# Reordering the first sample's loads, first norm and weight folds in a fused graph-network kernel

## The chip, the cores and the metric

The kernel runs on one core of a Trainium2 chip. The metric is the device time of one execution in microseconds (us), as the median of several runs: 2542.31 us before the change (three runs, 2541.89 to 2542.35). The profile is that of one such execution (2541.99 us, span in the trace 2540.2 us).

A core has five engines that run side by side: TensorE (matrix products; PE in the profile, PEld for its weight loads), VectorE (DVE), ScalarE (ACT), GpSimd (POOL) and SyncE (SP, which here only issues transfers). Transfers between the memory of the chip and the core's own buffers are done by 16 DMA engines; SP, ACT and POOL can each issue them on a queue of their own. Each engine works through its instructions in the order in which the program gives them, and waits where an operand or a buffer is not ready.

## The reference, cut to what matters

There are 16 samples, each with 1024 nodes of 128 features (`x`) and a dense adjacency matrix of 1024 x 1024 (`adj`), all in fp32. Two parts follow one another, each with a residual and a layer norm:

```python
def first(x, adj, W, b):                      # "first GNN"
    degree = adj.sum(-1)[:, :, None]
    nb = einsum('bid,bij->bjd', x, adj) / degree
    return relu(concat([x, nb], -1) @ W.T + b)

def layer(nodes, adj, ws, bs, wd, bd, wn, bn, wu, bu):
    src = einsum('bjv,bij->biv', nodes @ ws + bs, l2norm(adj, 2))   # rows scaled
    dst = einsum('bjv,bji->biv', nodes @ wd + bd, l2norm(adj, 1))   # columns scaled
    return tanh(concat([src, nodes @ wn + bn, dst], 2) @ wu + bu)

x = layernorm(x + first(x, adj, W, b))
y = x; # four such layers follow; the third and fourth also read earlier layers' inputs
x = layernorm(x + four_layers(y, adj, ...))
```

`l2norm(adj, 2)` divides each row by the root of its sum of squares, `l2norm(adj, 1)` each column. The layers' weights `ws`, `wd`, `wn` are multiplied with the parts of `wu` once ("folded"), so that messages come out of one product per layer.

## The kernel before

Samples are worked off one after another. While TensorE is in the layers of one sample, the next sample's adjacency is loaded, its sums of squares and degrees are taken, its columns and rows scaled and its first GNN and norm done. Sample 0 has nobody to hide behind: its loads, sums, first GNN and first norm stand at the start of the program, and the folding of the weights lies in its first layer. The last sample's final norm stands at the end. The change concerns these two ends and sample 0's first two layers.

The start: loads, then sums and gathers by pairs of row blocks (each pair is 1 MB, each of its four transfers 256 KB).

```python
load_pair(nc.scalar, PAIRS[0], range(G))
load_nodes(1)                                  # SP's queue
load_pair(nc.scalar, PAIRS[1], range(2))
load_pair(nc.sync, PAIRS[1], range(2, G))
load_nodes(0)
load_pair(nc.sync, PAIRS[2], range(G))
nc.sync.dma_start(w0n, w0)
nc.sync.dma_start(b0c, ...)
load_pair(nc.sync, PAIRS[3], range(G))
fetched = [fetch_weights(raw, 0, nc.sync, wm)]
rows = {...}                                   # rows 2, 3 of the adjacency once more, in another layout
fetched += [fetch_weights(raw, l, nc.sync) for l in range(1, NL)]
rows[0] = load_rows(0, 0, ...); rows[1] = load_rows(0, 1, ...)
make_identity(nc, ident)
# ...
for h in (1, 0):                               # transposes of x: both halves ahead of the gathers
    ...
for h, k in PAIRS[:-1]:
    for i in range(h * BPH + k, h * BPH + k + 2):
        square(i)                              # ScalarE, with the row's sum of squares
        degree(i)                              # VectorE, row sum
        if i != BPH:
            add_square(i)                      # GpSimd, adds squares for the column sums
        for h2 in (1, 0):
            gather(h2, i)                      # TensorE: matmul(pa[h2], xn[:, i], a[:, i, half(h2)])
```

The end of the first GNN and the first norm:

```python
def first_weights(b, h, xT, agT, yT, order=..., back=...):
    pw = product(f"pw0_{b}_{h}")
    by_halves(pw, w0T[:, 0], xT[:, s], True, False)
    by_halves(pw, w0T[:, 1], agT[:, s], False, True)
    nc.scalar.activation(order(yT[:, s]), back(pw), AF.Relu, bias=b0c)

degree_row(1)
with_x(1); with_x(0)                           # x into the norm's banks, by an identity product
square(first); square(second)                  # the last two row blocks, 2 and 3
for h in (1, 0):
    gather(h, first); gather(h, second)
degree(first); scaled(1); degree(second); degree_inverses(0)
add_square(first)
# power of the rows' sums of squares, on GpSimd
first_weights(0, 1, ...)
degree_row(0); scaled(0)
with_y(1)                                      # four small products add relu's result
first_weights(0, 0, ...)
stats = {1: norm_stats(pn[1], range(BPH), "0_0_1")}
fold_begin(0, fetched[0], nc.vector.tensor_copy)
with_y(0)
fold_end(0, fetched[0])
rinv = row_inverses(0, inv)
shift = norm_shift(stats[1], BPH, "0_0_1")
for q in range(BPH):
    norm_write_act(x1n[:, BPH + q], pn[1][:, q], stats[1], shift, q)
stats[0] = norm_stats(pn[0], range(BPH), "0_0_0")
add_square(second)
to_x1(1)                                       # transposes and a copy
for q in range(BPH):
    norm_write(x1n[:, q], pn[0][:, q], stats[0], q)
to_x1(0)

def norm_stats(pn, blks, name):
    for q in range(n):
        nc.vector.bn_stats(...); nc.vector.bn_aggr(...)
    nc.vector.tensor_scalar_add(ve, variance, LN_EPS)
    nc.gpsimd.tensor_tensor(rstd, ve, mhalf, ALU.pow)      # to the power -1/2
    return mv, rstd
```

Layer 1 of sample 0 runs on unscaled data and has hooks ahead of numbered steps. Steps 0 and 1 are own products, 2 to 17 the products with the columns, 18 to 33 those with the rows (`at`, which VectorE transposes from `rows`). Layer 2 has hooks too:

```python
hooks = {1: lambda *_: inverses(0, st0, NB), 3: rows0, 5: folded(1, fold_begin), 7: cinv0,
         9: folded(1, fold_end), 10: second0, 18: first0, 19: folded(2, fold_begin),
         22: folded(2, fold_end), 24: folded(3, fold_begin), 26: sums0, 29: folded(3, fold_end)}
# inverses: column sums from the parts, then their power on GpSimd; cinv0: that inverse as a row, by TensorE
# second0 ends, and first0 begins, with rows 0 and 1: scale_rows on ScalarE, transpose_rows on VectorE
# sums0: combine_1(y), finish(1), combine(2, y, T), combine_1(yt)

plain_layer(b, 0, ...)
wm = message_weights(b, 1)
a2 = load(n)             # the next sample's adjacency, into the buffer that the raw weights leave

# layer 2
def quarters2(b=b):
    if b == 0:
        combine(3, y, T); combine(2, yt, Q)
    for i in (3, 4):
        combine(i, yt, Q)
hooks = {0: quarters2}   # and sums(n, a2, st, (i,)) of the next sample at eight steps
if b == 0:
    hooks[20] = lambda: combine(4, y, T)
```

`fold_end(l)` ends with a transfer that saves the folded weights; `load(n)` waits until the last save has read the buffer. In `sums`, ScalarE squares a row block into one of two buffers and GpSimd adds it up.

The end of the program, the last sample's norm, first half in two pieces:

```python
shift = norm_shift(stats[1], BPH, ...)
for q in range(BPH):
    norm_write_act(o[:, BPH + q], pn["last"][:, q], stats[1], shift, q)
nc.sync.dma_start(ov[:, BPH:], o[:, BPH:])
for i in pieces:
    for q in range(2):
        nc.tensor.matmul(pn[i][:, q], f4[...], ident, start=False, stop=q == 1)
    stats[0] = norm_stats(pn[i], range(2), ...)
    for q in range(2):
        norm_write(o[:, i + q], pn[i][:, q], stats[0], q)
    nc.sync.dma_start(ov[:, i:i + 2], o[:, i:i + 2])
```

Of the kernel before, what the change touches and what calls it, by code (L numbers as in the profile page):

```python
# [23 lines left out]
def adj_resnorm_kernel(ctx: ExitStack, tc: tile.TileContext, x, adj, w0, b0, layers, out):  # L24
# [230 lines left out]
    def column_sums(b, state):  # L255

        tr = two.tile([P, N], F32, tag="sq", name=f"acct{b}")
        nc.vector.transpose(tr, state["acc"])  # L258
        part = two.tile([P, K], F32, tag="part", name=f"part{b}")
        nc.vector.reduce_sum(part, tr.rearrange("p (k r) -> p k r", r=C), axis=AX.X)  # L260
        state["part"] = part
# [114 lines left out]
    def norm_stats(pn, blks, name):  # L376
# [9 lines left out]
        rstd = two.tile([P, BPH], F32, tag="rst", name=f"rs{name}")  # L386
        nc.gpsimd.tensor_tensor(rstd[:, :n], ve[:, :n], mhalf[:, :n], ALU.pow)
        return mv, rstd

    def norm_write(dst, pn, stats, q):  # L390
        mv, rstd = stats
        nc.vector.tensor_scalar(dst, pn, mv[:, q, 0:1], rstd[:, q:q + 1], op0=ALU.subtract, op1=ALU.mult)

    def norm_shift(stats, n, name):
        mv, rstd = stats
        shift = two.tile([P, BPH], F32, tag="shift", name=f"sh{name}")
        nc.vector.scalar_tensor_tensor(shift[:, :n], mv[:, :n, 0], -1.0, rstd[:, :n], op0=ALU.mult, op1=ALU.mult)
        return shift

    def norm_write_act(dst, pn, stats, shift, q):  # L400
        nc.scalar.activation(dst, pn, AF.Identity, bias=shift[:, q:q + 1], scale=stats[1][:, q:q + 1])
# [23 lines left out]
    def first_weights(b, h, xT, agT, yT, order=lambda v: v, back=lambda v: v):  # L425
# [4 lines left out]
        nc.scalar.activation(order(yT[:, s]), back(pw), AF.Relu, bias=b0c)  # L430
# [4 lines left out]
    def load_rows(b, q, st):  # L435
# [3 lines left out]
        for g in range(G):  # L439
            for h in range(NH):  # L440
                nc.sync.dma_start(st[g * C:(g + 1) * C, :, h * P:(h + 1) * P], v[h, g])
# [266 lines left out]
    def load_nodes(h):  # L708
        for g in range(G):
            nc.sync.dma_start(xn[g * C:(g + 1) * C, h * BPH:(h + 1) * BPH], xv[h][g])  # L710

    load_pair(nc.scalar, PAIRS[0], range(G))
    load_nodes(1)
    load_pair(nc.scalar, PAIRS[1], range(2))
    load_pair(nc.sync, PAIRS[1], range(2, G))
    load_nodes(0)
    load_pair(nc.sync, PAIRS[2], range(G))
    nc.sync.dma_start(w0n, w0)
    nc.sync.dma_start(b0c, b0.rearrange("(p o) -> p o", o=1))
    load_pair(nc.sync, PAIRS[3], range(G))  # L720
    raw = Raw()
    wm = message_tile("wm1_0")
    fetched = [fetch_weights(raw, 0, nc.sync, wm)]
    Q = combined(0, "Q")
    rows = {q: load_rows(0, q, Q[i].rearrange("p k (u c) -> p (k u) c", u=2)) for i, q in ((2, 2), (3, 3))}
    fetched += [fetch_weights(raw, l, nc.sync) for l in range(1, NL)]
    rows[0] = load_rows(0, 0, Q[4].rearrange("p k (u c) -> p (k u) c", u=2))
    rows[1] = load_rows(0, 1, one.tile([P, 2 * NJ, HW // 2], F32, tag="T2", name="rows1_0"))

    make_identity(nc, ident)  # L730
# [9 lines left out]
    for h in (1, 0):  # L740
        pt = product(f"xtr0_{h}")
        for q in range(BPH):
            nc.tensor.transpose(pt[:, q * P:(q + 1) * P], xn[:, h * BPH + q], ident)
        nc.scalar.copy(nodes(xT[:, half(h)]), blocks(pt))

# [27 lines left out]
    for h, k in PAIRS[:-1]:  # L773
        for i in range(h * BPH + k, h * BPH + k + 2):
            square(i)
            degree(i)
            if i != BPH:
                add_square(i)
            for h2 in (1, 0):
                gather(h2, i)  # L780
    pt = product("w0tr")
    for k in range(2):
        nc.tensor.transpose(pt[:, k * P:(k + 1) * P], w0n[:, k * P:(k + 1) * P], ident)
    nc.scalar.copy(w0T.rearrange("p k v -> p (k v)"), pt[:, :2 * P])
    degree_inverses(1)
# [5 lines left out]
    pn = {}  # L791
# [4 lines left out]
    def scaled(h):  # L796
        nc.vector.tensor_mul(agT[:, half(h)], pa[h], dinv[:, half(h)])

# [16 lines left out]

    degree_row(1)
    with_x(1)
    with_x(0)
# [3 lines left out]
    for h in (1, 0):  # L822
        gather(h, first)
        gather(h, second)
    degree(first)
    scaled(1)
    degree(second)
    degree_inverses(0)
    add_square(first)
    nc.vector.tensor_scalar_max(cols[:, :NB], cols[:, :NB], NORM_EPS * NORM_EPS)  # L830
    nc.gpsimd.tensor_tensor(inv[:, :NB], cols[:, :NB], mhalf[:, :NB], ALU.pow)
    first_weights(0, 1, xT, agT, yT, blocks, nodes)
    degree_row(0)
    scaled(0)
    with_y(1)
    first_weights(0, 0, xT, agT, yT, blocks, nodes)
    stats = {1: norm_stats(pn[1], range(BPH), "0_0_1")}
    fold_begin(0, fetched[0], nc.vector.tensor_copy)
    with_y(0)
    fold_end(0, fetched[0])  # L840
    rinv = row_inverses(0, inv)
    shift = norm_shift(stats[1], BPH, "0_0_1")
    for q in range(BPH):
        norm_write_act(x1n[:, BPH + q], pn[1][:, q], stats[1], shift, q)
    stats[0] = norm_stats(pn[0], range(BPH), "0_0_0")
    add_square(second)
# [3 lines left out]
    to_x1(0)  # L850
# [12 lines left out]
    for b in range(B):  # L863
# [9 lines left out]
        if b == 0:  # L873
            for q in (2, 3):
                scale_rows(rows[q], q, rinv)
            t = messages(b, 0, feats, wm, {0: lambda: column_sums(0, st0)}, with_sums=False)
# [12 lines left out]
            def second0(destination, finish):  # L889
# [3 lines left out]
                for q in (0, 1):  # L893
                    scale_rows(rows[q], q, rinv)
# [9 lines left out]
            def sums0(destination, finish):  # L904
# [3 lines left out]
                combine_1(yt)  # L908

# [3 lines left out]
            hooks = {1: lambda *_: inverses(0, st0, NB), 3: rows0, 5: folded(1, fold_begin), 7: cinv0,  # L913
# [246 lines left out]
```

## Time and profile before

| what | value |
|---|---|
| median of three runs | 2542.31 us |
| span in the trace | 2540.2 us |
| TensorE busy | 2500.9 us, 98% |
| VectorE, ScalarE, GpSimd busy | 1646.4, 836.2, 506.2 us |
| moved by the DMA engines | 219.63 MB, mean 86 GB/s |
| SP's queue, ACT's queue | 361696 and 480 packets |
| one row of a 128 x 512 product in a full run of them (gather) | 0.43 us; each fp32 product has two such rows |
| addition of 128 x 1024 on GpSimd | 2.35 us |
| squares of 128 x 1024 on ScalarE, with their sum | 1.05 + 0.19 us |
| row sum of 128 x 1024 on VectorE | 1.22 us |
| power of 128 x 4 and 128 x 8 on GpSimd | 1.01 and 1.65 us |

How to read what follows: in the profile's lines "L771" is a line of the kernel. L771 is the gather, L179 `by_halves`, L490 the messages, L542 the products of layer 1, L669 those of the other layers, L813 the transposes of `to_x1`, L743 the transposes of `x`, L577 a copy of a finished bank on ScalarE, L478 `combine(4, ...)`. "out<-in" are the names of the program's tiles, "x24" is the number of rows merged into the line, and what stands in brackets is the idle time of the engine just before and what ended it. Times are from the start of the span.

### The profile page before, as it was taken

The numbers are of one execution on the slowest core, as the hardware profiler recorded it, in microseconds if no ns is written. First come the engines' busy times: TensorE is split into PE (matmuls) and PEld (weight loads), VectorE is DVE, ScalarE is ACT, GpSimd is POOL, SyncE is SP. The second block draws the span as 40 slices with busy tenths as digits, with TensorE's granted clock in tenths as the row PEclk, the third lists the DMA queues.
The fourth block names the chain that finished last, engine by engine and source line by source line (L and its number), as shares of the span: only waits on it lengthen the run. The fifth ranks groups of instructions, "written<-read, shape, count | busy, mean of one in ns | idle before, by whom it ended". The sixth has DMA issues, their size and how long they took to land.

```text
span 2540.2 us, 30180 instructions
## 1 busy us (share of the span) xinstructions
PE 2500.9 (98%) x11701; PEld 1155.8 (45%) x11701; DVE 1646.4 (65%) x1982; ACT 836.2 (33%) x1552; POOL 506.2 (20%) x192
## 2 busy tenths in 40 slices
PE   7999999999999999999999999999999999999998
PEld 4443545434454444544445444344544445444453
DVE  4657667576675856657576575766758567585643
ACT  4414324143331423315133241433414333142311
POOL 3311303013031120401213021130301203112000
PEclk9999999999999999999999999999999999999999
DMA  9416345172451715436154361634517245271410
GB/s 189 105 38 128 74 91 98 46 141 57 96 106 47 144 41 100 100 69 127 34 108 98 72 117 42 126 72 95 98 43 146 55 96 104 49 143 40 92 23 9
DMA packets 362319, 219.63 MB, mean 86 GB/s; under 512 B 148928, under 2 KB 333504, under 8 KB 362176
## 3 DMA queue, kind: packets, MB, share of 16 engines
q1 hardware_dynamic: 361696, 216.14, 42.0%
q10 hardware_dynamic: 480, 1.57, 0.3%
q8 instruction: 92, 1.51, 0.3%
q14 instruction: 51, 0.42, 0.1%
HBM read 199.17 MB, written 18.46 MB: 86 GB/s over the span
## 4 chain that ended last, share of the span: by engine, by line
PE 64%; DVE 9%; SPq 7%; DMA 7%; POOL 5%; ACT 4%; issue 3%; ACTq 0%; POOLq 0%; DVEq 0%
PE m L669 25%; PE z L669 17%; PE pt L490 9%; PE pa L179 8%; SPq L231 7%; DMA a<-in_adj_dram 4%; POOL acc L252 3%; PE pw L179 2%; POOL inv L292 2%; ACT sq L248 2%; DMA out_dram<-y 2%; DVE e L593 1%; ACT sq L245 1%; DVE acct L258 1%; DVE part L260 1%
## 5 line engine op out<-in xcount | busy, mean ns | idle before, releaser
L369 POOL TENSOR_TENSOR rs<-ve,mhalf 128x32 f32<-128x32 f32 x30 | 162.8, 5428 | 1388.4 <-DVE ve L367 1388.4
L669 PE MATMUL z<-at,t 128*64 128x512 f32 x1224 | 383.7, 592 | 0.0
L669 PE MATMUL m<-Q,S 128*64 128x512 f32 x768 | 339.3, 595 | 2.6 <-ACT e L577 2.6
L669 PE MATMUL m<-T,S 128*64 128x512 f32 x1008 | 290.9, 593 | 0.0
L493 DVE TENSOR_TENSOR t<-pt,wm 128x512 f32<-128x512 f32 x256 | 175.3, 690 | 174.1 <-PE pt L490 174.0
L669 PE MATMUL m<-a,t 128*64 128x512 f32 x1008 | 266.8, 594 | 0.0
L252 POOL TENSOR_TENSOR acc<-acc,sq 128x1024 f32<-128x1024 f32 x90 | 220.4, 2449 | 136.0 <-ACT sq L248 132.5
L669 PE MATMUL z<-a,S 128*64 128x512 f32 x504 | 230.1, 597 | 0.0
L669 PE MATMUL z<-T,t 128*64 128x512 f32 x504 | 226.8, 592 | 2.2 <-DVE T L478 2.2
L669 PE MATMUL z<-a,t 128*64 128x512 f32 x504 | 226.8, 592 | 0.0
L446 ACT ACTIVATE a<-a,rinv 128x256 f32<-128x256 f32 x480 | 198.2, 495 | 57.0 <-DMA a<-in_adj_dram 49.4
L669 PE MATMUL m<-at,t 128*64 128x512 f32 x828 | 214.6, 593 | 0.0
L327 DVE TENSOR_TENSOR a<-a,cinv 128x512 f32<-128x512 f32 x250 | 156.6, 698 | 88.1 <-DMA cinv<-dr 86.2
L490 PE MATMUL pt<-wm,f1T 128*128 128x256 f32 x768 | 213.4, 383 | 0.0
L179 PE MATMUL pa<-a,xn 128*64 128x512 f32 x960 | 208.6, 592 | 0.2 <-DVE e L592 0.2
L669 PE MATMUL z<-at,S 128*64 128x512 f32 x444 | 200.8, 592 | 0.0
L576 ACT COPY e<-m 64x512 f32<-64x512 f32 x63 | 36.7, 582 | 470.4 <-PE m L669 470.1
L669 PEld LDWEIGHTS m<-Q,S 128*64 128x64 f32 x768 | 105.5, 137 | 169.5 <-issue 149.2
L669 PEld LDWEIGHTS z<-at,t 128*64 128x64 f32 x1224 | 120.8, 137 | 130.4 <-issue 111.6
L669 PE MATMUL z<-Q,t 128*64 128x512 f32 x384 | 172.6, 592 | 0.0
L669 PEld LDWEIGHTS m<-T,S 128*64 128x64 f32 x1008 | 102.4, 137 | 144.4 <-issue 124.2
L490 PEld LDWEIGHTS pt<-wm,f1T 128*128 128x128 f32 x768 | 143.3, 190 | 44.0 <-issue 18.3
(189 smaller groups left out, 3675.7 us busy)
## 6 DMA issues: line engine op xcount, KB each, us to landing
a<-in_adj_dram SPq DMA_DIRECT2D x120, 512.0 KB, 12.9
a<-in_adj_dram SPq DMA_DIRECT2D x480, 128.0 KB, 4.2
xn<-in_x_dram SPq DMA_DIRECT2D x128, 64.0 KB, 2.1
wm<-wsave SPq DMA_DIRECT2D x16, 512.0 KB, 3.9
wm<-wsave SPq DMA_DIRECT2D x31, 256.0 KB, 3.1
xs<-in_x_dram SPq DMA_DIRECT2D x60, 128.0 KB, 3.5
cinv<-dr SPq DMA_DIRECT2D x30, 256.0 KB, 5.3
dinv<-dr SPq DMA_DIRECT2D x30, 256.0 KB, 5.2
```

Of the source, the lines that this page charges most:

```text
L179: nc.tensor.matmul(out[s], x[:, s], y, start=start, stop=stop)
L231: nc.sync.dma_start(ov[g, :, ks], ys[g * C:(g + 1) * C, ks])
L248: nc.scalar.activation(sq, a[:, i, :], AF.Square, accum_out=cols[:, i:i + 1])
L252: nc.gpsimd.tensor_add(acc, acc, sq)
L292: nc.gpsimd.tensor_tensor(inv[:, s], cols[:, s], mhalf[:, s], ALU.pow)
L327: engine.tensor_mul(a[:, i, s], a[:, i, s], cinv[:, s])
L369: nc.gpsimd.tensor_tensor(rstd, ve, mhalf[:, :n], ALU.pow)
L446: nc.scalar.activation(st[:, k], st[:, k], AF.Copy, scale=rinv[:, q * QB + k:q * QB + k + 1])
L490: nc.tensor.matmul(pt[:, q], f[:, i * P:(i + 1) * P], wm[:, 1 + c], start=(k == 0), stop=(k == nch - 1))
L493: nc.vector.tensor_add(t[j][:, o:o + 2].rearrange("p k a v c -> p k (a v c)"), pt, wm[:, 0][:, None, :].to_broadcast([P, 2, 2 * P]))
L576: nc.scalar.copy(e0[high], A[high])
L669: nc.tensor.matmul(o, x, y, start=start, stop=stop)
```

## The change

The loads of the first adjacency are halved between SP's queue and GpSimd's queue, all four pairs ahead of everything but the first weights and the nodes; the identity matrix, which GpSimd makes, comes after its eight transfers. Rows 2 and 3 follow with the weights, rows 0 and 1 are issued by GpSimd after the first norm's powers. On TensorE, the products that need only `x` stand ahead of the row blocks, undivided rather than by halves of the output. Folding of layers 2 to 4's weights begins earlier in layer 1, between the scalings of rows 0 and 1 on ScalarE. `combine(3, y, T)` moves from layer 2 into layer 1, and `combine(4, y, T)` from step 20 to step 12 of layer 2. The shift of the norm's writes on ScalarE is computed as minus the mean (VectorE) times the power's result (both on GpSimd). At the end, both pieces' statistics come ahead of their writes. It is meant to let TensorE start earlier, wait less in the first norm and in layer 2, and to shorten the tail. The diff, cut to its core:

```diff
-    load_pair(nc.scalar, PAIRS[0], range(G))
-    load_nodes(1)
     ...
+    nc.sync.dma_start(w0n, w0)
+    for p, pair in enumerate(PAIRS):
+        if p % 2 == 0:
+            load_nodes(1 - p // 2)
+        load_pair(nc.sync, pair, range(G // 2))
+        load_pair(nc.gpsimd, pair, range(G // 2, G))
+    make_identity(nc, ident)
     ...
+    for l, q in enumerate((2, 3, None, None)):
+        fetched.append(fetch_weights(raw, l, nc.sync, None if l else wm))
+        if q is not None:
+            rows[q] = load_rows(0, q, places[q])
     ...
+    to_xT(1)
+    with_x(1)
+    weights_of_x(1)                 # one 128x128 product, w0T[:, 0] with xT
+    for pair in PAIRS[:2]:
+        squares_of(*pair)
+        gathers_of(*pair)
+    nc.vector.tensor_add(sq[6], sq[6], sq[7])
+    add_square(5)
+    add_square(6)
+    to_xT(0)
+    with_x(0)
+    weights_of_x(0)
+    degree_inverses(1)
+    degree_row(1)
+    squares_of(*PAIRS[2])
+    gathers_of(*PAIRS[2])
+    add_square(0)
+    add_square(1)
     square(first)
     square(second)
-    for h in (1, 0):
-        gather(h, first)
-        gather(h, second)
+    gather(1, first)
+    gather(1, second)
     degree(first)
-    scaled(1)
     degree(second)
     degree_inverses(0)
+    degree_row(0)
+    gather(0, first)
+    gather(0, second)
+    scaled(1)
     add_square(first)
     ...
+    add_square(second)
+    weights_of_agT(1)               # w0T[:, 1] with agT, then relu
     scaled(0)
+    weights_of_agT(0)
     with_y(1)
     with_y(0)
+    stats = {1: norm_stats(pn[1], range(BPH), "0_0_1", True)}
+    fold_begin(0, fetched[0])
     fold_end(0, fetched[0])
+    stats[0] = norm_stats(pn[0], range(BPH), "0_0_0")
     for q in range(BPH):
+        norm_write_act(x1n[:, BPH + q], pn[1][:, q], stats[1], q)
+    for q in (0, 1):
+        rows[q] = load_rows(0, q, places[q], nc.gpsimd)
+    acct = column_transpose(0, st0)
     to_x1(1)
     ...                             # to_x1(0), row_inverses, column sums, scaling of rows 2, 3: after the first messages
-            hooks = {1: inverses, 3: rows0, 5: folded(1, fold_begin), 7: cinv0,
-                     9: folded(1, fold_end), 10: second0, 18: first0, 19: folded(2, fold_begin),
-                     22: folded(2, fold_end), 24: folded(3, fold_begin), 26: sums0, 29: folded(3, fold_end)}
+            hooks = {1: inverses, 3: rows0, 4: folded(1, fold_begin), 6: folded(1, fold_end),
+                     7: cinv0, 9: fold_and_scale(2, 0), 11: second0, 12: folded(2, fold_end),
+                     14: fold_and_scale(3, 1), 18: first0, 20: folded(3, fold_end), 26: sums0}
+            # sums0 ends with combine(3, y, T); fold_and_scale(l, q): fold_begin(l), then scale_rows(q)
-            hooks[20] = lambda: combine(4, y, T)
+            hooks[12] = lambda: combine(4, y, T)
     ...
+    for i in pieces:
+        ...                         # last products of the piece
+        stats[i] = norm_stats(pn[i], range(2), ...)
+    for i in pieces:
         for q in range(2):
+            norm_write(o[:, i + q], pn[i][:, q], stats[i], q)
         nc.sync.dma_start(ov[:, i:i + 2], o[:, i:i + 2])
```

## The prediction

> **What bounds the kernel now.** I read the shares of busy time first, then the waits of TensorE, then the order of time of the first 130 us and of the last 10 us.
>
> ```profile
> PE 2500.9 (98%) x11701; PEld 1155.8 (45%) x11701; DVE 1646.4 (65%) x1982; ACT 836.2 (33%) x1552; POOL 506.2 (20%) x192
> ```
>
> TensorE (PE) is busy for 2500.9 of 2540.2 us: only 39.3 us are left that reordering can win, plus time at a reduced clock. Where they lie is told by the list of TensorE's waits (sum in us, times, longest):
>
> ```profile
> PE xtr L743 <- DMA xn<-in_x_dram: 12.1, 2, 8.2
> PE rp L179 <- DVE sp L297: 6.0, 15, 0.4
> PE pc L179 <- DVE part L260: 4.9, 11, 0.8
> PE m L669 <- ACT e L577: 2.6, 1, 2.6
> PE z L669 <- DVE T L478: 2.2, 1, 2.2
> PE x1tr L813 <- DVE x1n L392: 1.5, 1, 1.5
> PE x1tr L813 <- ACT x1n L401: 0.9, 1, 0.9
> ```
>
> The rows that come 15 and 11 times belong to the steady state, which the change doesn't touch. All else happens once: 12.1 us for the first nodes, 2.4 us in the first norm, 4.8 us in layer 2 of sample 0. The rest, 7.8 us, is the tail: TensorE ends at 2532.4 (2531.21 + 1.16) and the span at 2540.2. So this is a change of microseconds in 2540, whatever it does.
>
> TensorE's order of time (start, length, what):
>
> ```profile
> 14.10 12.10 PE L771 MATMUL pa<-a,xn 128*128 128x512 f32 x24
> 28.41 3.60 PE L771 MATMUL pa<-a,xn 128*128 128x512 f32 x8
> 44.36 1.43 PE L813 MATMUL x1tr<-ident,x1n 128*128 128x128 f32 x4 [1.49 <-DVE x1n L392]
> 45.59 4.87 PE L490 MATMUL pt<-wm,x_T 128*128 128x256 f32 x16
> 50.29 1.02 PE L542 MATMUL z<-x_T,wown 128*128 128x512 f32 x2
> 112.61 0.81 PE L669 MATMUL m<-Q,S 128*64 128x512 f32 x1 [2.59 <-ACT e L577]
> 123.55 0.64 PE L669 MATMUL z<-T,t 128*64 128x512 f32 x1 [2.15 <-DVE T L478]
> ```
>
> Here x24 means 12 instructions: one fp32 matmul of 512 columns shows as two rows, 0.43 us each (x8 took 3.43 in the chain), so 0.86 us per matmul. From 13.2 to 40.6 us TensorE hardly rests: once the second node half has come at 13.2, the start is a queue of TensorE work, not of transfers. Layer 1 starts at 50.45 in the chain.
>
> A wait also costs clock. By stretch (after the core's number: stretch, length, busy times by engine, then granted clock, DMA share, GB/s):
>
> ```profile
> 46.00:48.00 2.00, 2.00 (x6) 1.62 (x5) 0.39 (x1) 2.00 (x6) 0.18 (x1) 0.50 0.77 225
> 114.00:115.00 1.00, 1.00 (x6) 0.33 (x4) 0.55 (x1) 0.97 (x3) 0.00 (x0) 0.50 0.00 0
> ```
>
> At half clock the 16 rows of pt take 4.87 us, against 3.69 for the same 16 at 90.08: 1.2 us lost. After the 2.6 us wait in layer 2, five paired steps take 3.89 us (112.61 to 116.50) where five at 0.43 take 2.15: 1.7 us lost.
>
> **What the Trainium skill says.** "DMA: Bandwidth & Descriptors", section "Issuing engines are not separate DMA queues": all queues end on the same 16 engines, so a second queue saves issue time, not bandwidth. The trace agrees: from 2 to 26 us the engines' share is 0.98 to 1.14 and the rate averages 210 GB/s, with two queues before 12 us and one after. The same page, "Latency and other measured facts", gives about 1 us to the first byte for transfers issued by GpSimd, put down to descriptors made by its own cores; no instruction here shows it, since GpSimd issues no transfer before. "TensorE: Matmul & The Clock Gate", "What's actually happening": the array drops to half clock after an idle window of about 3.4 us. The trace shows the halving, after a stretch that was only partly idle (40 to 44 us: 1.95 us busy of 4).
>
> **The change, part by part.**
>
> Loads. Needed before the last gather: adjacency 4.19 MB, nodes 0.52, first weights 0.13, together 4.85 MB. At 210 GB/s that is 23.1 us, and with about 2 us of start it ends at 25.2. Before, the last row block is waited for until 26.34, because weights and row blocks followed closely on the same engines. Worth 1.1 us there.
>
> First gathers. Now the transposes of one node half, its identity product and its weight product run ahead of the adjacency. The first pair lands when SP's queue has moved 0.92 MB (w0, nodes, half a pair) and GpSimd's about as much: 1.84 to 2.2 MB, about 11.5 us. Four matmuls per pair, partly at half clock: pair one until about 16.5, pair two 17 to 20.5. Then transposes 0.44, identity product 0.86, weight product 0.86, degree rows 0.43: 23.1. Pair three (3.4) to 26.5, two gathers (1.7) to 28.3, degree rows 28.7, two gathers 30.4. Before, they ended at 32.0.
>
> First norm. Before, after the gathers came x and aT products (1.89), Relu (0.70), four small products (1.16), the other half's 1.87, folds (1.7) and four more (1.00): the second half ends at 39.7. After: one aT product 0.86, Relu 0.7 overlapping the other product, then two times 1.0: halves end at 33.2 and 34.2. Statistics of half 1 on VectorE: 4 x 0.40 + 0.17 + 0.15, to 35.2; of half 0 to 37.0. GpSimd: power 1.01 and a small multiplication (estimate 0.3), to 36.5. ScalarE: fold copies to 36.7, four writes (1.51) to 38.2; transposes, copy 0.59, to 39.0; first pt product 0.91, to 39.9. VectorE meanwhile: transpose of the sums 1.24, four writes 1.37, to 39.7; then transposes, copy and the row inverses to 41.1, three pt products 2.7, to 43.8. TensorE again rests for most of 36 to 39, so I keep the half-clock loss of 1.2: layer 1 starts at 45.0 instead of 50.45. **Gain 5.4 us.**
>
> Layer 1. The same TensorE work in another order; the third fold ends about step 20 of 34 rather than 29. The next adjacency, whose buffer waits for the third weight save, so starts about 9 us earlier relative to layer 2 (before: save at 86.38, issue 89.07, first use 101.94). The price: one more combination (2.29) after layer 1's first half. VectorE then has 0.69 + 3 x 2.29 = 7.6 us in the 6.9 us of the last eight steps: loss about 0.3.
>
> Layer 2. Before, ScalarE begins the sums at 101.94, must wait 2.5 us for a buffer, and so reads the first bank at 111.4, when TensorE already waits. After, the sums begin about 9 us earlier relative to the layer: both the 2.6 us and the 1.7 us of half clock go. T4 moves from hook 20 to 12, ahead of reductions and reads on VectorE: the 2.2 us go. **Gain 2.6 + 1.7 + 2.2 - 0.3 = 6.2 us.**
>
> Tail. Two pieces ran as statistics, power, write, statistics, power, write; now the second statistics lie beside the first power. Second statistics from 2532.95, power to 2534.8, write to 2535.55 instead of 2537.28. **Gain 1.7 us.**
>
> New wait. 16 transfers of 128 KB now stand in GpSimd's order between the norm's power (to 38.1) and the column power that layer 1's step 7 needs. That step comes about 52.8 (45.0 + 1.9 + five steps 4.3 + fold 1.6). From about 1 us each, an estimate from the page cited, I take 0.9: GpSimd is free at 52.4, and the power (1.65) ends at 54.05. **Loss about 1.0**, with no loss of clock counted.
>
> Sum: 2542.3 - 5.4 - 6.2 - 1.7 + 1.0 = 2530.0; I put it at 2530.5, for small waits I have not seen.
>
> **The rivals.** First, GpSimd becomes the new wait. At 1.3 us per transfer the column power ends at 38 + 20.8 + 1.65 = 60.5, TensorE stands 7 us or more and drops its clock, and at the start the identity matrix, which stands behind eight such transfers, delays the transposes: some 2538 to 2540. Against it: 20% busy, and idle 7.0 us before that power. At 0.5 us each there is no wait: 2528 or a little less. Second, the start stays bound by transfers: bytes don't shrink, TensorE only waits earlier, and the first gain falls to 2 or 3 us: about 2533. For it speaks that the first pair shares its queue with 0.39 MB of small rows; against it, that the post-gather chain is shorter in any case. Third, layer 2 keeps its waits, because sums still stand ahead of the reads on ScalarE and each needs a GpSimd addition (2.36 us): about 2536. The margin I count is 4 to 5 us. Fourth, it hides altogether: not likely, since these waits are TensorE's own and TensorE sets the end.
>
> **Range and chances.** The parts are nearly independent; only GpSimd's time per transfer can take most of it back, hence a longer upper side: 2524.5 to 2538. 2% would be 51 us, more than all of TensorE's idle time: same is almost sure.
>
> **What would show it.** Right: layer 1's first z near 45 us, no wait of m for e in sample 0, none of z for T, last write near 2535.5, gathers ended near 30.4. Wrong: TensorE's cinvp waiting for GpSimd's inv by several us, the first xtr waiting for the identity beyond 11 us, the last row block landing after 26.

## The result, and the profile after

| | median us | runs |
|---|---|---|
| before | 2542.10 (2540.72 to 2542.35) | 4 |
| changed | 2529.03 (2525.06 to 2530.13) | 4 |

The ratio is 0.9947, with a 95% interval of 0.993 to 0.9964: 13.1 us less, well inside "within 2%". The prediction stood at 2530.5. A second measurement of the same kernel gave 2529.79 against 2540.71 (ratio 0.995, 0.9936 to 0.9963), 10.9 us less. The profiled run is the fastest of the first four (2525.06 us), so its span (2523.3 us) must not be set against 2540.2; the stages can be.

The shares of busy time of the changed kernel:

```profile
PE 2498.0 (99%) x11693; PEld 1158.6 (46%) x11693; DVE 1652.3 (65%) x1982; ACT 836.5 (33%) x1553; POOL 523.8 (21%) x217
```

TensorE's busy time is 2.9 us less. The work is the same (eight instructions fewer, as products are no longer halved), and a product at half clock lasts longer and counts as busy, so I take this for clock won back; no run shows it by itself. The rest of the gain is idle time. TensorE's waits in the first 135 us of the changed kernel (sum, times, longest) show what went:

```profile
PE w0tr L757 <- POOL inv L746: 6.3, 1, 6.3
PE x1tr L832 <- ACT x1n L409: 1.9, 1, 1.9
PE xtr L752 <- DMA xn<-in_x_dram: 1.0, 1, 1.0
PE pt L498 <- ACT x_T L833: 0.7, 1, 0.7
PE rp L179 <- DVE sp L303: 0.6, 2, 0.4
PE wtr L147 <- ACT raw L148: 0.2, 1, 0.2
PE bm L151 <- ACT raw L148: 0.2, 1, 0.2
PE cinvp L281 <- POOL inv L298: 0.2, 1, 0.2
...
```

Lines have moved: L743 is now L752 (transposes of `x`), L813 is L832 (transposes of `x1`), L771 is L785 (gathers), L490 is L498 (messages), L542 is L550 (layer 1), L669 is L677 (other layers). (Where the list names inv for w0tr, it is GpSimd's last small piece behind the identity.) There is no wait of m for e and none of z for T any more. The 12.1 us for the nodes have become 6.3 for the identity matrix, which GpSimd makes behind its eight transfers, and 1.0 for the nodes. In the first norm 1.9 us for x1n and 0.7 for its copy remain. The new wait for GpSimd's column power is 0.2 us.

TensorE's order of time in the changed kernel (start, length, what):

```profile
12.63 7.34 PE L785 MATMUL pa<-a,xn 128*128 128x512 f32 x16
...
28.07 1.88 PE L785 MATMUL pa<-a,xn 128*128 128x512 f32 x4
...
37.60 1.38 PE L832 MATMUL x1tr<-ident,x1n 128*128 128x128 f32 x4 [1.90 <-ACT x1n L409]
39.66 1.36 PE L498 MATMUL pt<-wm,x_T 128*128 128x256 f32 x4 [0.67 <-ACT x_T L833]
...
42.41 3.54 PE L498 MATMUL pt<-wm,x_T 128*128 128x256 f32 x12
45.80 1.02 PE L550 MATMUL z<-x_T,wown 128*128 128x512 f32 x2
```

The gathers end at 29.95 (28.07 + 1.88), layer 1 starts at 45.80. The last message products took 3.54 us (12 rows that take 2.86 at full clock in another run below), at a reduced granted clock. A line of the next view has a stretch and its length, the busy times of PE, PEld, VectorE, ScalarE and GpSimd with their numbers of instructions, the granted clock as a share of full speed (0.61 and 0.54 here), the share of the 16 DMA engines, and GB/s.

```profile
40.00:42.00 2.00, 1.87 (x8) 1.22 (x6) 0.88 (x3) 0.09 (x1) 2.00 (x4) 0.61 1.13 250
42.00:44.00 2.00, 1.94 (x8) 1.64 (x9) 1.31 (x2) 1.75 (x5) 1.27 (x3) 0.54 1.08 146
```

For the comparison of kernels I cut every trace at the same places, read from TensorE's order of time. "End" is the end of the span; the tail begins with the first products into the last norm's banks ("on").

| kernel (us) | gathers end | layer 1's first z | layer 3's first product | from z to layer 3 | tail | from gathers' end to z |
|---|---|---|---|---|---|---|
| before | 32.01 | 50.29 | 127.13 | 76.84 | 13.43 | 18.28 |
| changed | 29.95 | 45.80 | 116.47 | 70.67 | 12.05 | 15.85 |
| changed, second profile | 30.33 | 47.36 | 117.65 | 70.29 | 11.99 | 17.03 |

The long middle is not touched by the change, but it isn't constant: from the second sample's column power (at 129.55 us in the changed kernel) to the last sample's the changed kernel took 2167.8 and 2173.1 us in its two profiles, and 2172.1 before. This spread of about 5 us is why single whole times are not set against each other below, and why stages are.

### The profile page after: what moved, and what is told of

It is laid out like the page before. It is cut to its first block, busy times and chain, and to the rows that moved or that the text cites. A ratio compares the mean times of both kernels' runs of the same rounds, so it can differ in the third digit from the quotient of the medians.

```text
span 2523.3 us, 30190 instructions
## 1 busy us (share of the span) xinstructions
PE 2498.0 (99%) x11693; PEld 1158.6 (46%) x11693; DVE 1652.3 (65%) x1982; ACT 836.5 (33%) x1553; POOL 523.8 (21%) x217
## 4 chain that ended last, share of the span: by engine, by line
PE 67%; DVE 9%; SPq 5%; POOL 5%; DMA 4%; issue 4%; ACT 4%; DVEq 0%; POOLq 0%; ACTq 0%
PE m L677 26%; PE z L677 19%; PE pt L498 10%; PE pa L179 8%; SPq L231 5%; DMA a<-in_adj_dram 3%; POOL acc L252 2%; PE pw L179 2%; POOL inv L298 2%; ACT sq L248 1%; DVE e L601 1%; DMA out_dram<-y 1%; POOL acc L250 1%; ACT sq L245 1%; DVE cols L247 1%
## 5 line engine op out<-in xcount | busy, mean ns | idle before, releaser
L677 PE MATMUL z<-at,t 128*64 128x512 f32 x1224 | 383.7, 592 | 0.0
L677 PE MATMUL m<-Q,S 128*64 128x512 f32 x768 | 337.4, 592 | 0.0
L677 PE MATMUL m<-T,S 128*64 128x512 f32 x1008 | 290.9, 593 | 0.0
L677 PE MATMUL m<-a,t 128*64 128x512 f32 x1008 | 266.6, 594 | 0.0
L677 PE MATMUL z<-a,S 128*64 128x512 f32 x504 | 228.3, 593 | 0.0
L677 PE MATMUL z<-a,t 128*64 128x512 f32 x504 | 226.8, 592 | 0.0
L677 PE MATMUL z<-T,t 128*64 128x512 f32 x504 | 226.8, 592 | 0.0
L677 PE MATMUL m<-at,t 128*64 128x512 f32 x828 | 214.5, 593 | 0.0
L498 PE MATMUL pt<-wm,f1T 128*128 128x256 f32 x768 | 213.6, 383 | 0.1
L677 PE MATMUL z<-at,S 128*64 128x512 f32 x444 | 200.8, 592 | 0.0
L677 PEld LDWEIGHTS z<-at,t 128*64 128x64 f32 x1224 | 120.8, 137 | 130.7 <-issue 111.3
L677 PEld LDWEIGHTS m<-Q,S 128*64 128x64 f32 x768 | 105.2, 137 | 164.3 <-issue 146.2
L677 PE MATMUL z<-Q,t 128*64 128x512 f32 x384 | 172.6, 592 | 0.0
L677 PEld LDWEIGHTS m<-T,S 128*64 128x64 f32 x1008 | 102.4, 137 | 144.4 <-issue 123.9
L498 PEld LDWEIGHTS pt<-wm,f1T 128*128 128x128 f32 x768 | 143.3, 190 | 44.3 <-issue 19.9
```

The costliest lines, as they stand in the source:

```text
L498: nc.tensor.matmul(pt[:, q], f[:, i * P:(i + 1) * P], wm[:, 1 + c], start=(k == 0), stop=(k == nch - 1))
L677: nc.tensor.matmul(o, x, y, start=start, stop=stop)
```

## The experiments

Ratios are to the kernel before, measured on the same chip as the variant. The groups had medians of before of 2540.71, 2540.18, 2543.76 and 2544.28 us.

**The changed kernel once more** (no edit).

> The changed kernel once more, unchanged. The median of the changed kernel is 2529.0 us, but its profiled run took 2525.1, and between the first and the last sample's column power that profile has 4.3 us less than the one before, where the change has no instruction. Theory (the middle varies from run to run): a second profile shows another figure for that stretch, and the median is 2528 to 2530. Rival (the change also makes the steady state faster): the stretch is again about 2167.8 us, against 2172.1 before.

Measured: 2529.79 us, ratio 0.995 (0.9936 to 0.9963). The stages are the table's third row: the same waits in layer 2 are gone, the tail is the same to 0.1 us, the first norm is 1.2 us longer. In this profile the clock stood at 0.50 from 40 to 44 us instead of 0.61 and 0.54. So the 4 us by which the first profile's whole time lay lower are not a property of the change.

**Only the hooks of layers 1 and 2**, on the kernel before:

```diff
-    5: folded(1, fold_begin), 7: cinv0, 9: folded(1, fold_end), 10: second0, ...
+    4: folded(1, fold_begin), 6: folded(1, fold_end), 7: cinv0, 9: fold_and_scale(2, 0), 11: second0, ...
+    # sums0 also does combine(3, y, T); quarters2 no longer does
-            hooks[20] = lambda: combine(4, y, T)
+            hooks[12] = lambda: combine(4, y, T)
```

> The kernel before with layer 1's and layer 2's hooks of the changed one (folds sooner between row scalings, both moved combinations), loads, first norm and tail as before. Theory (layer 2's two waits are cured by the earlier next adjacency and the moved combinations alone): TensorE's waits of m for e (2.6 us) and of z for T (2.2 us) and the half clock after them (1.7 us) are gone, less about 0.5 us in layer 1, so 6 us less: about 2536. Rival (they need the earlier first norm as well): 0 to 2 us less.

Measured: 2533.77 us, ratio 0.9971 (0.996 to 0.9982): 6.9 us less. From z to layer 3 it takes 70.29 us instead of 76.84: 6.55 less. Start (z at 49.63) and tail (13.49) are those of before.

**All but the hooks**: the changed kernel with before's hooks and combinations.

> The changed kernel with layer 1's and layer 2's hooks of the one before. Theory (the parts add): the first norm's 4.7 us and the tail's 1.4 us stay, layer 2's waits come back: about 2536. Rival (the parts depend on each other, for example because the earlier start of layer 1 now meets rows that have not come): anything above 2539.

Measured: 2536.57 us, ratio 0.9983 (0.9976 to 0.999): 4.1 us less. Layer 1 starts at 45.53, and layer 2's two waits are back:

```profile
109.12 0.64 PE L677 MATMUL m<-Q,S 128*64 128x512 f32 x1 [2.20 <-ACT e L585]
120.04 1.12 PE L677 MATMUL z<-T,t 128*64 128x512 f32 x1 [3.84 <-DVE T L486]
```

The number in brackets is TensorE's idle time just before. The wait for T is larger than the 2.15 us of before, cinvp waits 1.4 us, and from z to layer 3 it takes 80.66 us, 3.8 more than before: of the 4.8 us by which layer 1 starts earlier, 0.9 are left at layer 3 (126.19 against 127.13). By whole times hooks and rest add up, 6.9 + 4.1 = 11.0 against 10.9 for the whole change in the same group; by stages they do not, since up to layer 3 the hooks alone win 7.2 us, the rest alone 0.9 and both 10.7 and 9.5 in the two profiles. In the profiles the earlier start is kept only with the new hooks. The medians leave room for more: of the 4.1 us the tail has 1.4.

**Only the tail**, on the kernel before: both pieces' statistics ahead of both writes.

> The kernel before with both pieces' statistics ahead of their writes in the tail and nothing else. Theory (prediction): the second power no longer stands behind the first writes, last write 1.7 us sooner. The changed kernel's profile shows about 1.4 us (from the transposes of the last norm to the end 12.05 us, before 13.43): about 2540.7. Rival (the transfer at the end hides it): no difference.

Measured: 2539.14 us, ratio 0.9993 (0.9984 to 1.0001), so the whole time doesn't settle it. The stage does: the tail takes 11.88 us instead of 13.43, 1.55 less.

**The hooks taken apart.** First only the folds, with combinations where they were; then only `combine(4, y, T)` at step 12 (`hooks[20]` becomes `hooks[12]`).

> The kernel before with the changed order of folds and row scalings in layer 1 only; both combinations stay in layer 2 (T4 at step 20). Theory A (two separate waits): the next adjacency comes about 9 us earlier, the wait of m for e (2.6 us, and 1.7 us of half clock) goes, the wait of z for T (2.2 us) stays: about 4 us less. Theory B (the second wait follows from the first, since VectorE's queue ahead of T4 waits for ScalarE's late reads): both go, about 6.5 us less, and moving the combinations adds nothing.

> The kernel before with T4 at step 12 instead of 20 of layer 2 and nothing else. Theory A: the wait of z for T goes (2.2 us less), that of m for e (2.6 us) stays. Theory B: the wait of z for T goes too, but since ScalarE's reads are what is late, something else of layer 2 waits in its place, and less than 1 us is won.

The folds alone: 2535.81 us, ratio 0.9982 (0.9976 to 0.9989), 4.4 us less. The wait of m for e is gone, that of z for T stays, in TensorE's waits as

```profile
PE z L669 <- DVE T L478: 1.7, 1, 1.7
```

T4 alone: 2540.09 us, ratio 0.9999 (0.999 to 1.0008): nothing. The wait of z for T is gone, and the other has grown from 2.6 us, at half clock afterwards (1.11 us for one row, against 0.64 behind the shorter wait above):

```profile
113.62 1.11 PE L669 MATMUL m<-Q,S 128*64 128x512 f32 x1 [4.35 <-ACT e L577]
```

T4 at step 12 runs while the next adjacency's sums are under way: VectorE's combination (2.28 us, from 105.50) now lies beside GpSimd's addition, which takes 4.22 us, where it took 2.36 in the kernel before:

```profile
105.77 4.22 POOL L250 TENSOR_TENSOR acc<-sq,sq 128x1024 f32<-128x1024 f32 x1 [34.50 <-ACT sq L248]
106.62 2.36 POOL L250 TENSOR_TENSOR acc<-sq,sq 128x1024 f32<-128x1024 f32 x1 [34.60 <-ACT sq L248]
```

(The first line is T4 alone, the second before.) ScalarE waits 4.4 us for this addition instead of 2.5, and reads the bank later. So the two waits are not independent terms. The earlier combination pays only after the folds have brought the adjacency forward.

**One queue for the first adjacency**: `load_pair(nc.sync, pair, range(G))`, and nothing on GpSimd's queue before rows 0 and 1.

> The changed kernel with all of the first adjacency on SP's queue. In the profiles the two-queue kernels moved 261 to 298 GB/s from 8 to 16 us, those before 202 to 214. Theory Q (two queues of long rows move more than one): about 205 GB/s from 8 us on, the last row block lands after 25.5 instead of 23.5 to 24, gathers end 1 to 2 us later. Theory P (the prediction's: the rate is that of the shared engines, whatever the queues): same landing, no difference beyond 0.5 us in the end of the gathers.

Measured: 2528.51 us, ratio 0.9953 (0.9938 to 0.9968): as fast as two queues. Busy times by stretch, of the changed kernel first:

```profile
8.00:12.00 4.00, 3.95 (x8) 1.90 (x8) 0.00 (x0) 0.59 (x1) 0.00 (x0) 1.00 1.04 287
12.00:16.00 4.00, 3.92 (x9) 1.64 (x8) 2.34 (x2) 2.19 (x4) 1.13 (x1) 1.00 1.04 294
```

and of the kernel with one queue:

```profile
8.00:12.00 4.00, 3.10 (x6) 0.87 (x5) 1.84 (x2) 1.84 (x3) 0.00 (x0) 1.00 1.05 213
12.00:16.00 4.00, 2.70 (x7) 1.06 (x6) 1.33 (x2) 1.19 (x3) 2.34 (x1) 1.00 1.12 218
```

The DMA engines are at work all the time in both (1.04 to 1.12), mostly on the same rows of 4 KB, and moved 287 and 294 GB/s against 213 and 218. The edit changes only the queue that issues half of the transfers. "DMA: Bandwidth & Descriptors", section "Issuing engines are not separate DMA queues", lets a second issuing engine save only the time to issue; here the transfers themselves ran a third faster, and the measurement decides. But two queues by themselves don't do it. In the kernel before, SP's and ScalarE's queues moved 0.53 and 0.31 MB between 12 and 16 us, and together no more than one queue:

```profile
12.00:16.00 4.00, 2.78 (x7) 1.78 (x8) 1.10 (x1) 3.52 (x6) 0.00 (x0) 1.00 1.06 210
```

By the order of their transfers both were then writing the same half of the 128 partitions (a tile's first dimension), 0 to 63; one queue works off the four groups of 32 partitions one after another. In the changed kernel SP's queue writes partitions 0 to 63 and GpSimd's 64 to 127 at the same time. So the higher rate came where both halves were written at once; whether one queue that alternates between the halves would reach it, no run shows.

The higher rate wins nothing in the whole. With two queues the identity and the nodes stand behind or beside the row blocks, the first gather runs at 12.63, and from there to 29.95 TensorE hardly rests, so faster blocks wait for it. With one queue the first gather runs at 10.19, TensorE waits 3.3 us for blocks, and the gathers end at 31.1. Layer 1 starts at 46.05, against 45.80 and 47.36: of the 1.15 us lost at the gathers 0.9 come back in the norm. The first row blocks are there earlier, so GpSimd is through with its additions earlier, and VectorE's small sum is not held up:

```profile
32.29 2.37 POOL L774 TENSOR_TENSOR sq<-sq,sq 128x1024 f32<-128x1024 f32 x1
36.00 1.02 POOL L398 TENSOR_TENSOR rs<-ve,mhalf 128x4 f32<-128x4 f32 x1 [1.34 <-DVE sh L397]
```

The power starts 4.9 us after the gathers' end, against 5.8 in the changed kernel, and TensorE waits 1.0 us for x1n, not 1.9.

**ScalarE's queue in place of GpSimd's**: `load_pair(nc.scalar, pair, range(G // 2, G))`.

> The changed kernel with ScalarE's queue in place of GpSimd's for half of the first adjacency. Theory Q: the rate is again over 260 GB/s, since two queues of long rows are what matters; but ScalarE issues transfers ahead of its own work and its first copy comes late, as before (there it was held to 12.3 us), so the first products start later and the gathers end 1 to 3 us later. Theory S (the rate comes from descriptors made by GpSimd): about 205 GB/s as before.

Measured: 2537.32 us, ratio 0.9988 (0.9981 to 0.9995), 8.8 us more than with one queue in the same group. ScalarE's order of time begins:

```profile
0.74 14.57 ACTq L714 DMA_DIRECT2D a<-in_adj_dram  x8
15.34 1.28 ACT L758 ACT_TABLE_LOAD   x1 [15.34 <-DMA xn<-in_x_dram]
```

The eight transfers hold ScalarE until 15.3, since its own work stands behind them. TensorE waits 7.7 us for the first copy of x_T and layer 1 starts at 53.89. GpSimd's own eight transfers hold it for 4.38 us and delay the identity matrix, at a time when it has little else to do. The rate, 242 and 256 GB/s from 8 to 16 us, is neither the 205 of the one theory nor the "over 260" of the other: both miss.

**The last addition of squares on VectorE.** In the changed kernel GpSimd adds row block 3 just ahead of the norm's first power. GpSimd's order of time there:

```profile
33.30 2.34 POOL L775 TENSOR_TENSOR sq<-sq,sq 128x1024 f32<-128x1024 f32 x1
35.75 1.02 POOL L398 TENSOR_TENSOR rs<-ve,mhalf 128x4 f32<-128x4 f32 x1
...
38.60 4.68 POOL L449 DMA_DIRECT2D Q<-in_adj_dram  x8
...
52.53 1.67 POOL L298 TENSOR_TENSOR inv<-cols,mhalf 128x8 f32<-128x8 f32 x1
```

The addition ends at 35.64, the power starts behind it. VectorE's small addition that the power also needs, in VectorE's order of time, ends at the same moment:

```profile
34.61 1.06 DVE L392 TENSOR_SCALAR ve<-mv 128x4 f32<-128x4 f32 x1
```

```diff
-    add_square(second)                                           # GpSimd
     weights_of_agT(1)
     scaled(0)
+    nc.vector.tensor_add(sq[4], sq[4], sq[second])
```

> The changed kernel with one edit: the last addition of squares (row block 3) is done by VectorE behind scaled(0), instead of by GpSimd ahead of the norm's first power. In the changed kernel GpSimd's addition runs from 33.30 to 35.64, the first norm power starts at 35.75, and VectorE's 128x4 addition ahead of it takes 1.06 us instead of 0.17. Theory A (the addition holds up the first norm, by GpSimd's order and by the access to the buffers that both engines share): the 128x4 addition takes 0.17 to 0.2, the power starts at 34.7 to 34.9, TensorE's wait of x1tr for x1n falls from 1.9 to about 0.9, layer 1's first z comes 0.9 to 1.2 us earlier relative to the gathers' end (15.9 instead of 16.9 at equal clock), time about 2528. Theory B (the path runs through the second half's norm, VectorE and the half clock, not through this power): the power moves but z does not, by less than 0.4 us; the time stays at 2529.

Measured: 2529.38 us, ratio 0.995 (0.9937 to 0.9962). The small addition takes 0.17 us again, which agrees with "SBUF — State Buffer", section "Who interferes with whom": of the two pairs of ports that VectorE has, GpSimd shares one, the instruction that comes first keeps it to its end, and of VectorE's instructions only those that use it wait. (The statistics beside the same addition, 0.27 us each, were not held up.) The power starts at 35.48. In this profile the gathers ended at 30.58, 0.63 us later than in the changed kernel's, so relative to them the power comes 0.9 us earlier. TensorE's wait for x1n is 1.0 us instead of 1.9, and the clock stays full:

```profile
40.00:42.00 2.00, 1.39 (x12) 1.05 (x11) 0.90 (x3) 0.59 (x1) 2.00 (x5) 1.00 1.06 181
```

From gathers' end to z it takes 13.90 us instead of 15.85: about 1 us is the wait, the rest goes with the clock. But now TensorE waits for GpSimd's column power, which stands behind sixteen transfers:

```profile
PE cinvp L281 <- POOL inv L298: 1.1, 1, 1.1
```

**Products that only keep the clock.** The changed kernel with three 128x512 products whose result is left unread: two behind `fold_end(0)`, one behind `to_x1(1)`.

> The changed kernel with three more products of 128x512 whose result nobody reads: two on TensorE behind the first fold, where it waits 1.9 us for x1n, and one behind the first transposes of x1, where it waits 0.67 us. Theory A (the idle stretch from 36 to 40 costs the clock, and the half clock from 40 to 43.4 costs 1.2 us or more): the granted clock from 40 to 44 is 0.9 to 1.0 instead of 0.54 to 0.61, the 12 rows of pt ahead of z take about 2.7 instead of 3.54, layer 1's first z comes 1.0 to 1.7 us earlier after the gathers' end, time 2527.5 to 2528. Theory B (two or three products are too little for the clock, or the time until z is set by VectorE and ScalarE): clock and z unchanged, or z later by up to 0.5 us as the products stand in the way; 2529 to 2529.5.

Measured: 2531.04 us, ratio 0.995 (0.9936 to 0.9963). The clock is 1.00 from 30 to 46 us, the 12 message rows take 2.86 us instead of 3.54, and from gathers' end to z it takes 14.81 us instead of 15.85. In the whole time nothing of it is seen; cinvp waits 1.2 us in this kernel, too.

**Four edits joined**: the addition on VectorE, one unread product at each place, three of four transfers of pairs 0 and 2 on GpSimd's queue with the identity matrix behind the first three, and rows 1 issued behind the column power.

> The changed kernel with four edits that the earlier runs point to. GpSimd's queue takes three of the four transfers of pairs 0 and 2, because SP's queue carries the nodes ahead of them, and the identity matrix is made behind the first pair's transfers; VectorE does the last addition of squares; two unread products fill TensorE's idle time in the first norm (one and one); rows 1 are issued by GpSimd behind the column power. If the queues' balance sets the arrival of the first pair: first gather at 9.5 to 10.5 instead of 12.63, gathers ended at 27.5 to 28.5 instead of 29.95, and with 1 us from the addition and 1 us from the clock, layer 1's first z at 41.5 to 43 and 2525.5 to 2526.5 in all, with the wait of cinvp for GpSimd's inverse below 1 us. If the first pair is bound by the engines' rate from the first descriptor on: first gather at 12 and later, z at 44, 2527.5 to 2528. If column power or rows become the wait: cinvp or the rows' products wait 1 to 4 us, and the time is that of the changed kernel.

Measured: 2529.89 us, ratio 0.9949 (0.9936 to 0.9961). The loads miss: first gather at 11.74 instead of 12.63, but the nodes' other half, behind SP's part of the first two pairs, now lands late, and TensorE stands:

```profile
20.98 0.63 PE L754 MATMUL xtr<-ident,xn 128*128 128x128 f32 x4 [2.21 <-DMA xn<-in_x_dram]
```

The clock falls after it, and the gathers end at 32.77, later than before the change. The rest does as expected: 13.90 us to z, no wait of cinvp, 70.30 us from z to layer 3.

**Addition and rows**, with the changed kernel's loads:

```diff
-    for q in (0, 1):
-        rows[q] = load_rows(0, q, places[q], nc.gpsimd)
+    rows[0] = load_rows(0, 0, places[0], nc.gpsimd)
+            def inverses0(destination, finish):          # hook 1 of layer 1
+                inverses(0, st0, NB)                     # column power on GpSimd
+                rows[1] = load_rows(0, 1, places[1], nc.gpsimd)
```

> The changed kernel with two edits: the last addition of squares on VectorE, as in after_vector_add, and rows 1 issued by GpSimd behind the column power instead of ahead of it; loads as in the changed kernel. In after_vector_add TensorE's cinvp waited 1.1 us for GpSimd's column power, which ended at 53.83 behind the sixteen transfers. Theory A (the wait is GpSimd's order, so the microsecond won in the first norm is given back there): the power runs at about 46.5 to 48.2, the wait of cinvp is gone, and from layer 1's first z to layer 3's first product it takes 70.3 to 70.7 us instead of 71.64; first z at 44 to 45; about 2527.5 in all. Theory B (rows 1 arrive too late for their scaling, or another wait takes its place): cinvp does not wait but the stretch stays at 71 to 72 us, with a wait for at or Q in layer 1; about 2529. Differences of one microsecond in the whole time lie within the spread of the middle of the program (4 us between single runs), so the verdict is read from the stages.

Measured: 2531.22 us, ratio 0.9948 (0.9934 to 0.9961). GpSimd's order is now

```profile
46.25 1.66 POOL L298 TENSOR_TENSOR inv<-cols,mhalf 128x8 f32<-128x8 f32 x1 [4.54 <-DVE cols L297]
47.88 4.66 POOL L449 DMA_DIRECT2D rows<-in_adj_dram  x8
```

The power waits for its operand (4.54 us, in brackets) and for no transfer, and runs six microseconds earlier. TensorE's cinvp doesn't wait, and from z to layer 3 it takes 70.30 us. From gathers' end to z it is 14.94 us this time: the wait for x1n is 1.0 us, as in after_vector_add, but the clock was 0.50 from 40 to 42 us, so the addition wins its microsecond each time and the one of the clock only sometimes. Layer 1 starts at 44.22, layer 3 at 114.52, 2 to 3 us ahead of the changed kernel's two profiles; but the gathers, which the edit doesn't touch, ended at 29.28 here, 0.7 to 1.0 us earlier than there. From gathers' end to layer 3 it is 85.24 us, against 86.52 and 87.32. The whole time doesn't show it. The middle takes 2174.5 us here, and 2177.6 in the profile of after_vector_add. TensorE's waits between 130 and 2480 us tell why whole times scatter; of the changed kernel

```profile
PE rp L179 <- DVE sp L303: 4.9, 13, 0.4
PE pc L179 <- DVE part L266: 2.5, 7, 0.6
PE pa L179 <- DVE e L600: 0.2, 1, 0.2
```

and of after_vector_add

```profile
PE rp L179 <- DVE sp L303: 5.5, 14, 0.4
PE pc L179 <- DVE part L266: 5.0, 8, 0.8
PE pa L179 <- DVE e L600: 4.1, 4, 1.8
```

Of the 9.8 us between the two middles, 7 are such waits. Whether the start shifts them or chance does, one profile of each can't say, and I leave it open. No variant beats the changed kernel by more than its interval.

## Why the prediction was right, point by point

**The sum.** Predicted 5.4 + 6.2 + 1.7 - 1.0 = 12.3 us. By stages: from the span's start to z 4.5 and 2.9 us in the two profiles, from z to layer 3 6.2 and 6.55 (the new wait is in it), tail 1.4; together 12.0 and 10.9, against 13.1 and 10.9 in the whole times. Time and sum held, in part by luck: the first norm came 0.9 to 2.5 us short of its 5.4, while the stretch from z to layer 3, for which 6.2 - 1.0 = 5.2 were forecast, gave 1.0 to 1.3 more. (The 5.4 sets a forecast of 45.0 against 50.45 of one view; TensorE's order of time has 50.29, which makes 0.16 us of the miss.)

**The loads.** Two steps were wrong and made up for each other. "At 210 GB/s" is the rate of one queue; two queues moved 287 to 294 GB/s for eight microseconds, and the last row block was there at 23.47 and 24.04 instead of 25.2. (The prediction's "two queues before 12 us and one after" was misread, too: in the kernel before, both queues moved data until 17 us.) And the first pair landed at 12.6, not at 11.5, because the small rows of the nodes stood ahead on SP's queue: in after_joined, with only one of the pair's four transfers behind them, its first square runs at 11.2. The gathers ended at 29.95 and 30.33, predicted 30.4: luck, as the two misses cancel. From the first gather on TensorE is the limit, and so it hides the rate.

**The first norm: the term that was mis-sized.** Predicted 5.4 us, measured 4.5 and 2.9. What failed is "statistics of half 1 on VectorE: 4 x 0.40 + 0.17 + 0.15, to 35.2" and the power after it: the 0.17 took 1.06, since GpSimd was adding row block 3; and the power, behind that addition in GpSimd's own order, could not begin before 35.64 in any case. I had counted GpSimd's queue for the transfers but not for the addition that the diff moved ahead of the norm. After_vector_add gives 0.9 us of it back, and after_one_queue, where the additions are done earlier, shows the same 0.9. The other part is the clock: the 1.2 us that I kept was right in kind (after_warm wins 1.0 us, by clock alone) but varies with the run: from 40 to 42 us it was 1.00 in after_vector_add, 0.50 in after_add_and_rows, whose code is the same up to there, and 0.61 and 0.50 in the changed kernel's two profiles.

**Layer 2.** Predicted 2.6 + 1.7 + 2.2 - 0.3 = 6.2; before_hooks alone took 6.55 off the stretch. The sums begin at 90.12 instead of 101.94, and the read for which TensorE had waited runs at 101.04 instead of 111.97; the product that needs it starts at 105.43 without a wait. What was wrong is the independence of the terms: T4's 2.2 us exist only once the 2.6 are gone (before_t4: nothing; before_folds: 4.4 us; both with the third combination: 6.9).

**The tail.** Predicted 1.7, measured 1.4 and 1.4, and 1.55 in before_tail. The second statistics came where expected, and the last write ended 0.25 us later than forecast; 0.17 of it is the step from VectorE's addition (ends at 2518.65) to GpSimd's power (2518.82), which had been left out.

**The new wait.** Predicted 1.0 us at a start of layer 1 at 45.0; measured 0.2 at 45.80, none at 47.36, 1.1 at 44.48 (after_vector_add). The step is right, and for a partly wrong reason. A transfer costs GpSimd 0.55 to 0.59 us, not 0.9 (4.68 us for eight): the 0.9 had come from a time to the first byte, which is not the time that the issuing engine spends; from 38.60 to 52.53 it is sixteen times 0.585, or 9.4 us, and the other 4.5 us GpSimd spends waiting for landings, because most of rows 1's transfers wait for one of rows 0. The power ended at 54.2, predicted 54.05. The wait and the first norm's loss are the same microsecond: as the norm was late, the wait was hidden. By stages: from gathers' end to layer 3 the changed kernel took 86.52 and 87.32 us, after_vector_add 85.54, after_add_and_rows, without the wait for the column power but at half clock, 85.24, and after_joined, without both, with two unread products and at full clock from there on, 84.20. So the addition by itself keeps about half of what it won, and the rest came only with the rows moved, too.

**The rivals.** GpSimd as the bound did not come (it stays the next wait in line). "The start stays bound by transfers" is not what happened: after_one_queue has a quarter less rate between 8 and 16 us and the same time. The second profile's 2.9 us lie within this rival's "2 or 3 us", but it is the norm and the clock that made them so few, as its gathers ended at 30.33. Two parts of the rival are true: the first gather waits for its pair (12.6), and at the lower rate TensorE waits 3.3 us for blocks. "Layer 2 keeps its waits" is half right for T4 by itself, and wrong for the whole change.

## What to carry to other kernels

A move of a microsecond is read from stages cut at the same instructions in both traces, not from whole times that scatter by more. Before counting the gain of an earlier start, ask what stands next in line: here the norm's lateness hid GpSimd's column power, and layer 2's wait for e hid that for T, so a repair alone won half or nothing. An instruction moved to another engine's order has to be counted there as well: one addition on GpSimd cost TensorE one microsecond of waiting.

## What the hardware showed that I had not expected

- Transfers of (mostly) 4 KB rows moved 287 to 294 GB/s when SP's queue wrote one half of the partitions and GpSimd's the other, and 213 to 218 on one queue, with the DMA engines at work all the time in both. With ScalarE's queue for GpSimd's it was 242 and 256. Two queues that wrote the same half, in the kernel before, moved 210. One queue alternating between the halves was not run.
- ScalarE was held for 14.57 us by eight transfers of 256 KB, GpSimd for 4.38 us.
- Beside an addition on GpSimd, VectorE's 128x4 addition took 1.06 instead of 0.17 us, and a 128x2048 combination 4.33 instead of 2.29 us. It goes the other way, too: in before_t4, beside VectorE's combination GpSimd's 128x1024 addition took 4.22 instead of 2.36 us.
